# When the norms of the next units are made: at the end of a turn, or between its exponentials

## The chip, the cores and the metric

The kernel runs on one core of a Trainium2 chip. The core has five engines that work side by side, each through its own queue of instructions in a fixed order: TensorE (PE in the profile, matrix products), VectorE (DVE), ScalarE (ACT), GpSimd (POOL) and SyncE (SP, which here only starts DMAs). An instruction that waits holds up all that stands behind it in its own queue, and nothing in the others. The metric is the device time of one execution in microseconds (us); lower is better.

## The reference, cut to what matters

Two layers work on x, 8 sequences of 128 tokens with 512 features, in float32. The first is an adapter matrix chosen per sequence and a small mixture of low-rank experts. The second is attention over a paged cache of keys and values, followed by a router over 64 experts. Nearly all the time goes to the attention:

```python
q = jnp.einsum('bsd,ed->bse', x, Wq).reshape(bsz, seqlen, HQ, D)     # 32 heads of 128
k = jnp.einsum('bsd,ed->bse', x, Wk).reshape(bsz, seqlen, HK, D)     # 8 heads
...
q = _rmsnorm(q, q_norm_w)      # t * rsqrt(mean(t * t) + EPS) * w
k = _rmsnorm(k, k_norm_w)
...
q = _rope(q, pos)
k = _rope(k, pos)
...
scores = jnp.einsum('bqhd,bkhd->bhqk', q, k_all) * SCALE     # 512 cached keys and 128 new ones
scores = jnp.where(valid[:, None, None, :], scores, -1e+30)
probs = jax.nn.softmax(scores, axis=-1)
o = jnp.einsum('bhqk,bkhd->bqhd', probs, v_all)
```

The change is about the norms: for each query and key head the sum of squares over 128 features, and from it the factor `(mean + eps) ** -0.5`.

## The kernel before, in words

**Units and turns.** The attention is cut into 64 units: one sequence and one key head, with its four query heads. `iteration(u)` is one turn of the main loop, for u = 0 to 66, and works on several units at once, as a pipeline: it makes the scores and the softmax of unit u, the norms and the rotation of unit u + 3, the product with the values of unit u - 2 and the output product of unit u - 3. In between it makes the projections (queries, keys, values) of units further ahead. Four consecutive turns belong to one cycle of projections: in odd turns four products, in even turns three. In turns with u%4 = 2 the products of that turn complete unit u + 3 itself.

The order on each engine is written out by hand: the program is under a manual schedule, and each engine runs its instructions in the order in which the code issues them. The semaphore waits between engines follow from the tiles that the instructions share.

**One turn, by engine.** For each of the four heads h of unit u:

- TensorE makes `scores` (L798 against the cached keys, L801 against the new ones), then one output product of unit u - 3 (L902, into y), then a projection (L259).
- VectorE makes the masked maximum `mask_exp` (L811, from PSUM, scaled by the norm's factor `rs`), later the reciprocal of the softmax sum (L827) and the 32x32 block transpose of the normalized head (`blocks`, L833, into pb). It also adds the projection products (L262).
- ScalarE makes the exponential (L822, with the sum `den`).
- GpSimd multiplies with the reciprocal (`normalize`, L828). In the loop, `normalize(u, h - 1)` follows `mask_exp(u, h)`, so a head is normalized one step after its exponential, and `blocks(u, h - 2)` follows one step later.

**The end of a turn.** After the loop over heads come, in the order of the code: `add_output` (ya, L919 or L923), the mask of the next step, `heads_qk` (ScalarE, L867), the weight loads of some turns on GpSimd's queue (`load_q` L153, `load_o` L177), `normalize(u, 3)`, then `norms(u + 3)`, then the last two `blocks`, `exchange_out(u)` and `rotate(u + 3)`.

- `norms` has five squares on ScalarE (L308, one for each head, with its accumulator read), a copy of the values, vn (L310), and on GpSimd ss (L312, scale and add) and rs (L314, the power -0.5). There is one line for each: the profile names the tiles sq, vn, ss and rs.
- `exchange_out` sends the transposed blocks through DRAM (px), with two DMAs from SyncE's queue and two from ScalarE's (L847). In the next turn `exchange_in` fetches them back (qkb and pT, L857 and L860, SyncE). On SyncE's queue the rest of the key pages of the next step (kt, L194) stands behind that.
- `rotate` multiplies with the tables (L326, four query heads), and then the key head with its factor rs (L340), on VectorE; its result is transposed with the next unit's blocks (L784).
- In the next turn ScalarE begins with `evict_o` (oT, L891), the copy of the attention output of unit u - 2 out of PSUM, which TensorE needs for the first y product of that turn.

Some turns carry more: weight sums on VectorE in turns with u%16 from 10 to 13 (L163), weight loads on GpSimd's queue with u%16 = 8 to 11 (`load_q`, two DMAs each) and 12, 13 (`load_o`), four subtractions of x on GpSimd after turns 2, 5, 7 and 9 (`sums_x`). From turn 59 on the router of the finished sequences runs along (`f_turn`, a ScalarE copy at L686 behind the third exponential, and `f_gate`).

Of the kernel before, what the change touches and what calls it, by code (L numbers as in the profile page):

```python
# [9 lines left out]
F32 = mybir.dt.float32  # L10
# [6 lines left out]
P = 128  # L17
B = 8
# [5 lines left out]
D = 128  # L24
HKV, REP = 8, 4
NH = REP + 1
# [31 lines left out]
def adaln_ffn_kernel(  # L58
# [163 lines left out]
    pj = ctx.enter_context(tc.tile_pool(name="pj", bufs=1))  # L222
    units = [(st, st // B * GH + j) for st in range(NQ * B) for j in range(GH)]
    NU = len(units)
# [73 lines left out]
            )  # L298
        nc.scalar.copy(c_t[u][:, c * HW : (c + 1) * HW], ps)

    def norms(u):

        cs, b = c_t[u], units[u][0] % B
        ss = pj.tile([P, NH], F32, tag="ss", name=f"ss_{u}", bufs=5)
        sq = pj.tile([P, D], F32, tag="sq", name=f"sq_{u}")
        for h in range(NH):
            at = h // 2 * HW + h % 2 * D if h < REP else 2 * D
            nc.scalar.activation(sq, cs[:, at : at + D], AF.Square, accum_out=ss[:, h : h + 1])  # L308
        vn = pj.tile([P, D], F32, tag="vn", name=f"vn_{u}", bufs=6)
        nc.scalar.activation(vn, cs[:, 2 * HW - D :], AF.Copy, scale=down[:, b : b + 1])  # L310
        vn_t[u] = vn
        nc.gpsimd.tensor_scalar(ss, ss, 1.0 / D, eps[:, b : b + 1], ALU.mult, ALU.add)  # L312
        rs = pj.tile([P, NH], F32, tag="rs", name=f"rs_{u}", bufs=5)
        nc.gpsimd.tensor_tensor(rs, ss, mhalf, ALU.pow)  # L314
        rs_t[u] = rs
# [436 lines left out]
    with ExitStack() as l1:  # L752
# [223 lines left out]
        def iteration(u):  # L976

            on = lambda v: 0 <= v < NU
            fb = LAST.get(u)
            r, group = u % 16, (u // 16 + 1) * GH  # L980
            f = room(fb) if fb is not None else None

            if u % 4 == 3:
                k, j, four = (u + 5) // 4, 0, True
            elif u % 4 == 0:
                k, j, four = (u + 4) // 4, 0, False
            elif u % 4 == 1:
                k, j, four = (u + 3) // 4, 1, True
            else:
                k, j, four = (u + 2) // 4, 1, False  # L990
            slots = ()
            if 2 < u and k < NU // 4:
                slots = (1, 2, 6) if four else (4, 5, 3)
            st = u // GH
            pages = on(u) and 1 < st + 1 < NQ * B
            first, end = ((0, 10), (10, NPP))[u % GH]
            if pages:
                gather(st + 1, first, first + 3)
            if on(u - 1):
                exchange_in(u - 1)  # L1000
            if pages:
                gather(st + 1, first + 3, end)
            if pages:
                gather_v(st + 1, u % GH * LC // GH, (u % GH + 1) * LC // GH)
            if on(u + 3) and u % GH == 1:
                make_tables(units[u + 3][0])
            if u % GH == 0 and B <= st - 1 < NQ * B:
                load_y(st - 1)
            if on(u - 3):
                evict_o(u - 3)  # L1010
            if u >= NU and fb is not None:
                yT_t[fb] = f_turn(fb, *f)
            if u > NU:
                z = u - NU - 1
                z_turn(z, bank("q" if z else "kv", f"ztp_{z}"), lambda n, shape: y_home[
                    z
                ].rearrange("p (c s) -> p c s", c=NC))
            for h in range(REP):
                if on(u):
                    scores(u, h)  # L1020
                    mask_exp(u, h)
                    if h > 0:
                        normalize(u, h - 1)

                    if h == 1:
                        if u == 2:
                            rotate(4)
                        elif u == 3:
                            sums_q(1, 3, 2)
                        elif u == 4:  # L1030
                            sums_q(1, 4, 1)
                        elif r in (10, 11, 12, 13) and u < NU - 8:
                            sums_q(group + r // 12, *((3, 2), (4, 1))[r % 2])
                    if h == 2:
                        new_pb(u)
                        if u + 2 in range(3, NU):
                            blocks_qk(u + 2, u)
                    if h > 1:
                        blocks(u, h - 2)
                    if h == 1 and u == NU - 5:  # L1040
                        f_fold(f[1])
                    if h == 2 and fb is not None:
                        yT_t[fb] = f_turn(fb, *f)
                if on(u - 3):
                    output(u - 3, h)
                if h > 0 and slots:
                    project(k, j, slots[h - 1 : h])

                if (u, h) in WHOLE:
                    project_whole(1, *WHOLE[u, h])  # L1050
            if on(u - 3):
                add_output(u - 3)
            if on(u + 1) and (u + 1) % GH == 0:
                make_mask(units[u + 1][0])
            if u + 1 in range(3, NU):
                heads_qk(u + 1)

            if u < NU - 8:
                if r in (8, 9, 10, 11):
                    load_q(group + r // 10, r % 2, r % 2 + 2)  # L1060
                if r in (12, 13):
                    load_o(group, r % 2 * 2, r % 2 * 2 + 2)
            if 16 < u < NU and r in (1, 2):
                load_o(group - 1, r * 2 - 2, r * 2)
            if NU - 8 < u < NU - 2:
                f_weights(u - NU + 7)
            if u == 2:
                sums_q(0, 1)
            if on(u):
                normalize(u, REP - 1)  # L1070
            if u == 0:
                norms(4)
            elif 4 < u + 3 < NU:
                norms(u + 3)
            if on(u):
                blocks(u, REP - 2)
                blocks(u, REP - 1)
                exchange_out(u)
            if 4 < u + 3 < NU:
                rotate(u + 3)  # L1080
                if four and slots:
                    project(k, j, (7,))

            if u in (2, 5, 7, 9):
                sums_x({2: 2, 5: 3, 7: 0, 9: 1}[u])
            if u == NU - 14:
                t = wp.tile([P, 4 * DM], F32, tag="wo", name="y_home", bufs=GH + 1)
                y_home.update({b: t[:, b * DM : (b + 1) * DM] for b in range(4)})
            if u == NU - 6:
                rooms()  # L1090
            if fb is not None:
                f_gate(fb, *f_project(fb, yT_t.pop(fb), *f), *f)
            if on(u - 2):
                values(u - 2)
# [160 lines left out]
```

## Time and profile before

| | |
|---|---|
| time, median of 3 runs | 1243.18 us (1242.82 to 1249.42) |
| profiled execution, its own time | 1245.7 us |
| its span in the profile | 1243.9 us |
| TensorE busy | 1225.7 us (99%) |
| VectorE busy | 901.9 us (73%) |
| GpSimd busy | 590.9 us (48%) |
| ScalarE busy | 506.5 us (41%) |
| granted TensorE clock, mean | 0.998 |
| squares (L308), with reads | 98.8 + 59.7 us on ScalarE, 320 each |
| rs (L314) | 99.5 us on GpSimd, 64 instructions, 1554 ns mean |

A line of the timeline has the start and the duration in us, the engine, the line of the program, the operation, the tile written and the tiles read, the shape and the number of instructions; in brackets, the idle time before it and what ended it. A line of the waits has who waited (engine, tile, line), for whom, the total in us, how often, and the longest. "ACTq" and "SPq" are DMAs started from the queues of ScalarE and SyncE. An instruction's end, start plus duration, can lie a little past the start of the next one on its engine, because they are pipelined. Turns are counted by the masked maxima (L811), four to a turn; turn 20 starts at 439.47 us in this execution.

### The profile page before, as it was taken

The numbers are of one execution on the slowest core, as the hardware profiler recorded it, in microseconds if no ns is written. First come the engines' busy times: TensorE is split into PE (matmuls) and PEld (weight loads), VectorE is DVE, ScalarE is ACT, GpSimd is POOL, SyncE is SP. The second block draws the span as 40 slices with busy tenths as digits, with TensorE's granted clock in tenths as the row PEclk, the third lists the DMA queues.
The fourth block names the chain that finished last, engine by engine and source line by source line (L and its number), as shares of the span: only waits on it lengthen the run. The fifth ranks groups of instructions, "written<-read, shape, count | busy, mean of one in ns | idle before, by whom it ended". The sixth has DMA issues, their size and how long they took to land.

```text
span 1243.9 us, 15998 instructions
## 1 busy us (share of the span) xinstructions
PE 1225.7 (99%) x3847; PEld 651.1 (52%) x3847; DVE 901.9 (73%) x2045; ACT 506.5 (41%) x1457; POOL 590.9 (48%) x687
## 2 busy tenths in 40 slices
PE   8999899999999999999999999999999999999998
PEld 7765455554555555545555545554555555555444
DVE  3546788888877777788877777788777777777522
ACT  1334444444444444444444444444444444443211
POOL 2443565576544444565545545555555444543100
PEclk9999999999999999999999999999999999999999
DMA  8822777788877887788878878888888877787512
GB/s 302 304 78 94 229 234 245 245 274 281 269 243 245 272 258 239 259 295 278 269 248 267 264 221 258 294 272 267 257 268 262 255 243 233 246 261 269 179 51 85
DMA packets 205505, 298.99 MB, mean 240 GB/s; under 512 B 84643, under 2 KB 117156, under 8 KB 204516
## 3 DMA queue, kind: packets, MB, share of 16 engines
q1 hardware_dynamic: 173812, 205.58, 52.6%
q10 hardware_dynamic: 18720, 52.32, 12.0%
q0 software_dynamic: 12880, 40.08, 9.7%
q8 instruction: 31, 0.51, 0.2%
q14 instruction: 62, 0.51, 0.1%
HBM read 183.54 MB, written 114.36 MB: 239 GB/s over the span
## 4 chain that ended last, share of the span: by engine, by line
PE 89%; DMA 4%; DVE 2%; ACT 1%; issue 1%; POOL 1%; SPq 1%; ACTq 0%; DVEq 0%; POOLq 0%
PE o L880 19%; PE p L259 19%; PE y L902 17%; PE s L798 16%; PE s L801 4%; PE bp L517 2%; PE op L1147 2%; PE p L292 2%; PE cp L495 2%; PE fz L701 2%; DMA kt<-in_kc 1%; DMA bww<-in_base_w 1%; DMA px<-pb 1%; PE cp L512 1%; DMA pT<-px 1%
## 5 line engine op out<-in xcount | busy, mean ns | idle before, releaser
L828 POOL TENSOR_SCALAR p<-p,den 128x640 f32<-128x640 f32 x256 | 211.8, 827 | 424.4 <-DVE den L827 423.8
L822 ACT ACTIVATE p<-p,low 128x640 f32<-128x640 f32 x256 | 211.9, 828 | 436.3 <-DVE den L827 295.6
L811 DVE CUSTOM_DVE_ANT_0 p<-s,mask,rs 128x640 f32<-128x640 f32 x256 | 223.5, 879 | 108.8 <-PE s L801 106.1
L259 PE MATMUL p<-wqkv,xo 128*128 128x384 f32 x784 | 280.5, 487 | 0.0
L902 PE MATMUL y<-wo,oT 128*128 128x512 f32 x512 | 262.8, 598 | 7.6 <-ACT oT L891 7.4
L798 PE MATMUL s<-kt,qkT 128*128 128x512 f32 x504 | 258.9, 595 | 1.5 <-DVE low L811 0.8
L880 PE MATMUL o<-pT,vt 128*128 128x512 f32 x512 | 230.2, 593 | 0.0
L833 DVE STREAM_TRANSPOSE pb<-p 128x640 f32<-128x640 f32 x256 | 211.0, 824 | 16.9 <-POOL p L828 16.9
L259 PEld LDWEIGHTS p<-wqkv,xo 128*128 128x128 f32 x784 | 149.1, 190 | 139.8 <-issue 72.3
L801 PEld LDWEIGHTS s<-qkT 128*128 128x128 f32 x504 | 96.2, 191 | 121.0 <-issue 121.0
L880 PEld LDWEIGHTS o<-pT,vt 128*128 128x128 f32 x512 | 97.5, 190 | 110.1 <-issue 95.0
L204 POOL DMA_INDIRECT vt<-in_vc,vrow x128 | 136.3, 1065 | 37.4 <-issue 28.2
L798 PEld LDWEIGHTS s<-kt,qkT 128*128 128x128 f32 x504 | 95.4, 191 | 96.7 <-issue 54.0
L308 ACT ACTIVATE sq<-c 128x128 f32<-128x128 f32 x320 | 98.8, 309 | 8.1
L314 POOL TENSOR_TENSOR rs<-ss,mhalf 128x5 f32<-128x5 f32 x64 | 99.5, 1554 | 5.3
L801 PE MATMUL s<-qkT 128*128 128x128 f32 x504 | 97.2, 275 | 0.0
L891 ACT COPY oT<-o 128x512 f32<-128x512 f32 x64 | 37.4, 585 | 144.9 <-PE o L880 133.6
L902 PEld LDWEIGHTS y<-wo,oT 128*128 128x128 f32 x512 | 78.6, 192 | 14.2 <-ACT oT L891 9.7
L262 DVE TENSOR_TENSOR c<-c,p 128x384 f32<-128x384 f32 x84 | 45.3, 539 | 28.8 <-PE p L259 28.7
L880 PE MATMUL o<-pT,vn 128*128 128x512 f32 x128 | 65.4, 592 | 0.0
L308 ACT ACTIVATION_READ_ACCUMULATOR sq<-c 128x1 f32 x320 | 59.7, 187 | 0.0
L340 DVE SCALAR_TENSOR_TENSOR ca<-c,rs,tab 128x128 f32<-128x128 f32 x64 | 24.8, 387 | 45.1 <-POOL rs L314 45.1
(181 smaller groups left out, 1200.7 us busy)
## 6 DMA issues: line engine op xcount, KB each, us to landing
pT<-px SPq DMA_DIRECT2D x64, 1280.0 KB, 6.7
px<-pb ACTq DMA_DIRECT2D x120, 400.0 KB, 5.3
px<-pb SPq DMA_DIRECT2D x120, 400.0 KB, 5.5
qkb<-px SPq DMA_DIRECT2D x61, 320.0 KB, 3.5
kt<-in_kc SPq DMA_DIRECT2D x512, 32.0 KB, 4.4
wqkv<-in_wqkv POOLq DMA_DIRECT2D x32, 384.0 KB, 5.4
yd<-ya SPq DMA_DIRECT2D x24, 256.0 KB, 3.1
wo<-in_wo POOLq DMA_DIRECT2D x12, 512.0 KB, 4.7
```

Source lines behind the costliest of these rows:

```text
L204: nc.gpsimd.indirect_dma_start(out=kv_t[step][1][:, c, :], out_offset=None, in_=vc, in_offset=bass.IndirectOffsetOnAxis(ap=vrow[:, hf, at ...
L259: nc.tensor.matmul(out=ps, lhsT=xo[:, pr, x, c, :], rhs=w[:, c, :], start=(c == 0), stop=(c == 1))
L308: nc.scalar.activation(sq, cs[:, at : at + D], AF.Square, accum_out=ss[:, h : h + 1])
L314: nc.gpsimd.tensor_tensor(rs, ss, mhalf, ALU.pow)
L798: nc.tensor.matmul(out=s[:, :L], lhsT=qkT[:, h, :], rhs=kt[:, :, g % GH, :], start=True, stop=True)
L801: nc.tensor.matmul(out=s[:, L:NK], lhsT=qkT[:, h, :], rhs=qkT[:, REP, :], start=True, stop=True)
L811: nc.vector.tensor_tensor_reduce(out=p, in0=s_t.pop((u, h))[:, :NK], in1=mask_t[st], scale=rs_t[u][:, h : h + 1], scalar=BIG, op0=ALU.add, ...
L822: nc.scalar.activation(p, p, AF.Exp, bias=low, scale=-1.0, accum_out=den)
L828: nc.gpsimd.tensor_scalar(p_t[u, h], p_t[u, h], den, 1.0, ALU.mult, ALU.mult)
L833: nc.vector.transpose(pb_t[u][:, :, h * w : (h + 1) * w].rearrange("p i (j a) -> p j i a", a=32), p_t.pop((u, h)).rearrange("p (j i a) -> ...
L880: nc.tensor.matmul(out=o, lhsT=vt[:, c, j * D : (j + 1) * D] if c < LC else vn_t.pop(u), rhs=pT[:, c], start=(c == 0), stop=(c == LC),)
L902: nc.tensor.matmul(out=y_t[st], lhsT=oT_t[u][:, h, :], rhs=wo_t[g][:, h, :], start=(h == 0 and j == 0), stop=(h == REP - 1 and j == GH - 1),)
```

## The change

`norms` is split. `squares(u, first, end)` makes some of the five squares, and `norms(u, first)` makes the rest, vn, ss and rs. A flag `early` is set for turns u from 3 to 60 except those with u%4 = 2. In an early turn, three squares of unit u + 3 are issued behind the exponential of head 1, and the other two with vn, ss and rs behind that of head 2. Both stand ahead of the `normalize` call of that step, so on GpSimd ss and rs come between the normalizations of heads 0 and 1. In the turns with u%4 = 2, and outside the range, the norms stay at the end of the turn. No instruction is added or taken away, and the order on TensorE, VectorE and SyncE is the same as before; on ScalarE and GpSimd the moved instructions take their new places.

```diff
-    def norms(u):
-
-        cs, b = c_t[u], units[u][0] % B
-        ss = pj.tile([P, NH], F32, tag="ss", name=f"ss_{u}", bufs=5)
-        sq = pj.tile([P, D], F32, tag="sq", name=f"sq_{u}")
-        for h in range(NH):
+    ss_t = {}
+
+    def squares(u, first, end):
+
+        cs = c_t[u]
+        if first == 0:
+            ss_t[u] = pj.tile([P, NH], F32, tag="ss", name=f"ss_{u}", bufs=5)
+        ss = ss_t[u]
+        sq = pj.tile([P, D], F32, tag="sq", name=f"sq_{u}_{first}")
+        for h in range(first, end):
             at = h // 2 * HW + h % 2 * D if h < REP else 2 * D
             nc.scalar.activation(sq, cs[:, at : at + D], AF.Square, accum_out=ss[:, h : h + 1])
+
+    def norms(u, first=0):
+
+        squares(u, first, NH)
+        cs, b, ss = c_t[u], units[u][0] % B, ss_t.pop(u)
         vn = pj.tile([P, D], F32, tag="vn", name=f"vn_{u}", bufs=6)
...
+            early = 2 < u < NU - 3 and u % 4 != 2
...
                 if on(u):
                     scores(u, h)
                     mask_exp(u, h)
+
+                    if early and h == 1:
+                        squares(u + 3, 0, 3)
+                    elif early and h == 2:
+                        norms(u + 3, 3)
                     if h > 0:
                         normalize(u, h - 1)
...
             if u == 0:
                 norms(4)
-            elif 4 < u + 3 < NU:
+            elif 4 < u + 3 < NU and not early:
                 norms(u + 3)
```

## The prediction

> **What bounds the kernel now.** I read three views: the busy table, the list of waits, and one turn of the main loop instruction by instruction. The first two:
>
> ```profile
> PE 1225.7 (99%) x3847; PEld 651.1 (52%) x3847; DVE 901.9 (73%) x2045; ACT 506.5 (41%) x1457; POOL 590.9 (48%) x687
> ...
> PE y L902 <- ACT oT L891: 7.4, 8, 2.6
> ...
> DVE ca L340 <- POOL rs L314: 45.1, 59, 3.5
> ```
>
> TensorE is busy for 1225.7 of 1243.9 us, at a granted clock of 0.998. All its idle time is 18.2 us, and about half of that lies before the first turn and after the last. The waits to see: TensorE's largest is 7.4 us, in 8 pieces, for oT, the copy that ScalarE makes of the attention output. VectorE waits 45.1 us for rs, the result of the norms, but VectorE does not set the end. So the 45.1 us are worth at most what TensorE can recover: its stalls in turns 10, 26, 36, 44 and 59 are 0.73, 0.68, 0.96, 0.88 and 1.00, together 4.25 us, or 0.34%. The other question is whether the change makes TensorE wait where it doesn't now. Turn 20 (the iteration u = 20, without a stall), by engine: ScalarE and ACTq, TensorE, VectorE, GpSimd:
>
> ```profile
> 446.37 0.19 ACT L822 ACTIVATION_READ_ACCUMULATOR p<-p,low 128x1 f32 x1
> ...
> 453.05 0.84 ACTq L847 DMA_DIRECT2D px<-pb  x2
> 454.31 0.58 ACT L891 COPY oT<-o 128x512 f32<-128x512 f32 x1 [1.29 <-PE o L880]
> ...
> 455.19 1.02 PE L902 MATMUL y<-wo,oT 128*128 128x512 f32 x2
> ...
> 448.78 0.83 DVE L833 STREAM_TRANSPOSE pb<-p 128x640 f32<-128x640 f32 x1
> 450.02 0.56 DVE L262 TENSOR_TENSOR c<-c,p 128x384 f32<-128x384 f32 x1 [0.42 <-PE p L259]
> ...
> 451.10 0.15 DVE L827 RECIPROCAL den<-den 128x1 f32<-128x1 f32 x1
> ...
> 452.17 0.85 DVE L833 STREAM_TRANSPOSE pb<-p 128x640 f32<-128x640 f32 x1 [0.18 <-POOL p L828]
> ...
> 448.95 0.80 POOL L828 TENSOR_SCALAR p<-p,den 128x640 f32<-128x640 f32 x1 [2.45 <-DVE den L827]
> ```
>
> See the order on ScalarE at the turn's end: the exchange DMAs wait for the last block transpose (452.17), take 0.84, and behind them in the same queue stands oT, for which the y matmul at 455.19 waits. From the transpose: 0.88 to the DMAs, 0.88 more to where oT may start (453.93), but it starts at 454.31, when TensorE has finished o: 0.38 free. In turn 10, where y did stall, it began 0.64 after oT:
>
> ```profile
> 287.46 0.85 ACTq L847 DMA_DIRECT2D px<-pb  x2
> 288.35 0.58 ACT L891 COPY oT<-o 128x512 f32<-128x512 f32 x1 [1.17 <-PE s L801]
> ...
> 288.99 1.13 PE L902 MATMUL y<-wo,oT 128*128 128x512 f32 x2 [0.73 <-ACT oT L891]
> ```
>
> In turn 20 that would be 454.95, and y comes at 455.19: another 0.24 free. **An even turn therefore stands 0.62 us of delay of its last block transpose**; beyond that each tenth is TensorE time. An odd turn has one more product (1.29 us) ahead of o; in turn 9 its DMAs are out at 269.53 and oT starts at 271.30, so 1.77 us are free.
>
> **The change, part by part.** It adds no instruction and removes none. In turns 3 to 60 except those with u%4 = 2 (44 turns; 15 even, 29 odd) it moves 5 squares with 5 accumulator reads and the vn copy on ScalarE, and ss and rs on GpSimd. The queues of TensorE, VectorE and SyncE keep their order; the moved steps issue no DMA.
>
> *ScalarE.* A square with its read follows the next by 0.43 us, so three cost 1.30 after the second exponential, two and vn (0.39) cost 1.25 after the third. In turn 20 the second exponential ends at 443.32 and the third starts at 445.63 (2.3 us gap); the third ends at 446.56, the fourth starts at 449.16 (2.6 us gap). Both fit: nothing. In odd turns the copy of u (L265, 0.48) waits behind the three squares, about 1.1 us later; its reader at L262 comes 3.0 us after it today (turn 21): nothing. What the squares free at the end of the turn (2.1 us before the exchange DMAs) is gained only where ScalarE, not the transpose, held the DMAs: turn 59.
>
> *GpSimd, where the price is.* ss waits for the fifth square, and behind it now stand the normalizations of heads 1, 2 and 3, the weight DMAs, and behind those VectorE's transposes. In turn 20: third exponential read out at 446.56, two squares to 447.31, ss at 447.41 (0.10 later, as at the end of turns today), 0.27 long, rs 0.09 later, at 447.77. How long is rs in that place? The trace has it beside other work:
>
> ```profile
> 127.26 0.27 POOL L312 TENSOR_SCALAR ss<-ss,eps 128x5 f32<-128x5 f32 x1 [1.45 <-ACT sq L308]
> 127.61 1.18 POOL L314 TENSOR_TENSOR rs<-ss,mhalf 128x5 f32<-128x5 f32 x1
> ...
> 519.19 1.74 POOL L314 TENSOR_TENSOR rs<-ss,mhalf 128x5 f32<-128x5 f32 x1
> ```
>
> The first runs beside two masked maxima (L811), the second beside the two rotations L326, which have two inputs in SBUF. Ends: 1.18 and 1.75. In the new place it meets an L262 add and the fourth masked maximum, then an idle VectorE; no L326. I take 1.20. The Trainium skill, "SBUF — State Buffer", section "SBUF: two separate sides", says that GpSimd and such a two-input VectorE instruction take a shared port pair as a lock: the first to start keeps it for its whole length, the other is blocked. At 519.19 rs had started 0.03 before the first L326, yet the two L326 kept their pace (0.57 apart) and rs was drawn out by 0.54. So the measurement decides: beside L326 it is rs that pays. Were the fourth masked maximum, due at 447.90, held by rs as that rule has it, it would end at 449.77, and the transpose behind it would start at 449.85; by the rows it starts at 449.80. The sum is the same within 0.05.
>
> With 1.20, rs ends at 448.97 and head 1's normalization runs to 449.77 instead of 446.50. The transpose of head 1 (448.78) starts at 449.80, 1.02 late. It ends its 0.75 pitch at 450.55; the L262 add due at 450.02, where it had waited 0.42 for TensorE, is 0.53 late, and so are ya, the reciprocal (451.63), head 3's normalization (0.24 behind it, 0.80 long) and the last transpose: 452.70. Head 2's normalization is done at 450.57 and waits on nothing. **Delay of the last transpose 0.53, against 0.62: no stall, by 0.09.** Seven of the exchange DMA pairs took 0.88 to 0.96 instead of 0.84; I allow 0.3 us in all for edges like these.
>
> Then rotate: 452.70 + 0.77 + 0.57 + 0.68 = 454.72 for L340, no longer waiting for rs. Turn 24, which is regular, has it 15.22 after its first masked maximum, which in turn 20 is 454.69. The removed wait (about 0.5) is eaten by the added one.
>
> *Turns that differ.* u = 8, 24, 40: two weight DMAs (1.56 us) stand between the normalizations of heads 2 and 3. Turn 24: head 2 ends at 516.83, the DMAs at 518.36, head 3 at 519.21; last transpose 519.25 against 518.45, 0.80 late: 0.18 over, three times, +0.5. Turns 11 and 13, with weight sums on VectorE: 1.3 late, oT 0.15 to 0.18 later, inside 0.24: nothing. Turns 59 and 60 have another ScalarE copy (L686) behind the third exponential; it comes 1.25 late, its matmul had 0.6 to spare: +0.6 each. But turn 59's stall of 1.00 comes from squares, rs (1.67 us of VectorE waiting) and the gate behind it, and goes: together +0.2. Turn 9 ends with four GpSimd subtractions beside L340, which then takes 0.82 instead of 0.35; they start earlier now, and turn 10's stall may lose 0.3.
>
> *SyncE.* Its exchange DMAs come 0.5 to 1.3 later, and behind them in the next turn the last three K pages. Their landing against the first scores: 0.1 us to spare in turns 25 and 49, 1 to 4.6 in the other turns behind a moved even one where the trace shows it. At most 0.5 in each of the two: +0.6 as a middle. The transposed probabilities are needed 15 us after they land: nothing.
>
> **Sum:** 0.3 + 0.5 + 0.2 - 0.3 + 0.6 = +1.3 us. The profiled execution took 1245.7 us for a span of 1243.9; both grow alike, so I add it to the median, 1243.2: **1244.5 us**.
>
> **Rivals.** *Faster:* the early norms relieve turns 10, 26, 36, 44 and 59 of all 4.25 us, which gives 1239. For it: 45 us of VectorE waiting. Against: in 26, 36 and 44 the exchange DMAs are slow or wait for pages, which no norm changes. *Slower, by one mechanism:* rs stays near 1.75 in its new place (the profile's mean is 1.554, with L326 nearly always beside it). Then the last transpose is 1.03 late, and each even turn loses 0.41 (8 x 0.41), turns 8, 24, 40 0.74 each, turns 12, 28, 44 some 1.8 together, odd turns 11, 13, 29, 43 another 1.8, and turn 10 0.5 more: +9.6, 1252.8. It decides from rs above about 1.3 us. *Slower by pages:* with landings of 7.4 us, as in turn 49, in place of about 5, all 14 turns that follow a moved even turn lose about 0.5: 1250.
>
> **Chances.** Within 0.5% (6.2 us; runs of one kernel here spread by as much, 1242.82 to 1249.42): 0.79, my forecast, with the faster rival's 1239 inside it. Slower: 0.17, of which rs 0.11 and pages or what I don't see 0.06. Faster by over 0.5% needs more stalls removed than I can find: 0.04. Range 1240 to 1251: most of the faster rival, the page case, the lower part of the rs case.
>
> **What would show it.** Right: rs near 1.20 us; head 1's transpose waiting about 1 us for GpSimd in place of L340's wait for rs; the last transpose some 0.5 us later against y; TensorE's wait for oT still near 7 us. Wrong: rs at 1.6 or more, or y waiting for oT in most even turns, or scores waiting for pages.

## The result, and the profile after

The changed kernel takes 1251.09 us (median of 8 runs, 1249.23 to 1253.04) beside 1246.35 us for the kernel before, run alongside (8 runs, 1241.68 to 1249.42). The ratio is 1.0049, with a 95% interval of 1.003 to 1.0068. A second measurement gave 1.0057 (1.0037 to 1.0077). So the change costs about 0.5%, some 5 to 7 us, where 1.3 us were forecast. 1251.09 lies just above the range on record (1240 to 1251). The kernel before was itself 3.2 us slower in these runs than in the three shown ahead of the prediction. The difference is therefore the better measure of the forecast, and it is wrong by 3.4 us or more.

The profiled execution took 1249.23 us for a span of 1247.5, at a granted clock of 0.997. Before, these were 1245.7, 1243.9 and 0.998. The line numbers after are higher by 9 from `norms` on: the square is L312, rs is L323, the masked maximum is L820, `normalize` is L837, the block transpose is L842, the exchange is L856, oT is L900 and y is L911.

First the page of the changed kernel: the busy table, and from the costliest groups the two kinds of matmul that can wait at a turn's edge.

```profile
PE 1228.7 (98%) x3847; PEld 651.5 (52%) x3847; DVE 915.9 (73%) x2045; ACT 497.0 (40%) x1457; POOL 580.8 (47%) x687
...
L911 PE MATMUL y<-wo,oT 128*128 128x512 f32 x512 | 263.8, 600 | 6.4 <-ACT oT L900 6.4
L807 PE MATMUL s<-kt,qkT 128*128 128x512 f32 x504 | 258.9, 595 | 3.8 <-DMA kt<-in_kc 2.4
```

Then its list of waits, the two rows that the change exchanges, with the first of them as it was before, and the durations of rs in the view of that tile:

```profile
DVE pb L842 <- POOL p L837: 53.3, 103, 1.8
...
DVE ca L349 <- POOL rs L323: 13.1, 16, 3.7
```

```profile
DVE pb L833 <- POOL p L828: 16.9, 65, 2.2
```

```profile
L323 POOL TENSOR_TENSOR rs<-ss,mhalf x64: 1183/1197/1744, 66.8 to 1119.0; 128x5 f32<-128x5 f32 x64
```

The reader is to see three things. VectorE's wait for rs fell from 45.1 to 13.1 us, and its wait for a normalized head grew to 53.3 us (16.9 before). The median rs is 1.197 us (minimum, median and maximum stand in ns). And TensorE's wait for oT is 6.4 us, not more than the 7.4 of before. In this one execution it has a new wait instead, 2.4 us for key pages.

Turn 20 again, instruction by instruction; it starts at 441.36 us here. The last row is the first o matmul of the same turn before:

```profile
449.63 1.19 POOL L323 TENSOR_TENSOR rs<-ss,mhalf 128x5 f32<-128x5 f32 x1
...
450.83 1.57 POOL L837 TENSOR_SCALAR p<-p,den 128x640 f32<-128x640 f32 x2
...
451.66 0.84 DVE L842 STREAM_TRANSPOSE pb<-p 128x640 f32<-128x640 f32 x1 [0.91 <-POOL p L837]
451.71 3.60 PE L889 MATMUL o<-pT,vt 128*128 128x512 f32 x8
...
454.54 0.84 DVE L842 STREAM_TRANSPOSE pb<-p 128x640 f32<-128x640 f32 x1 [0.19 <-POOL p L837]
...
455.41 0.85 ACTq L856 DMA_DIRECT2D px<-pb  x2
...
456.31 0.59 ACT L900 COPY oT<-o 128x512 f32<-128x512 f32 x1 [4.00 <-PE o L889]
...
457.08 1.02 PE L911 MATMUL y<-wo,oT 128*128 128x512 f32 x2
```

```profile
449.82 3.60 PE L880 MATMUL o<-pT,vt 128*128 128x512 f32 x8
```

rs takes 1.19 and the two normalizations of heads 1 and 2 run behind it; head 1's transpose waits 0.91 for them. The last transpose starts 2.83 after the first o matmul; before it was 2.35 (452.17 less 449.82). It is 0.48 late. oT starts 4.60 after o where it was 4.49, and y doesn't wait. This is the chain of the prediction, with 0.48 for its 0.53.

Where, then, does TensorE lose the time? A turn is taken from the start of its last o matmul to that of the next: 15.92 us into an even turn and 17.21 into an odd one, when nothing waits. What is above that, in us, in the two profiled executions, is put down to the turn that it leads into, so that the stalls which the prediction names at the end of turns 10, 26, 36 and 44 stand here at 11, 27, 37 and 45:

| place | before | after |
|---|---|---|
| turn 3, while the pipeline fills | 5.32 | 6.47 |
| turns 9, 25, 41 (behind u = 8, 24, 40) | 0 | 0.79 |
| turns 12, 30, 38 (in after, waits for key pages) | 0.43 | 3.09 |
| turns 13, 29 (behind u = 12, 28; y waits for oT) | 0.24 | 1.06 |
| turns 11, 27, 37, 45, 58 (y waits for oT) | 4.67 | 3.96 |
| turns 59 and 60 | 3.45 | 2.79 |

What else turns 4 to 58 lose is 0.45 and 0.26 in all. The regular even turns have 0.00 in both. Turn 28, which leads into turn 29, is not regular: on VectorE it carries weight sums. After, then before:

```profile
584.74 3.60 PE L889 MATMUL o<-pT,vt 128*128 128x512 f32 x8
...
588.11 0.84 DVE L842 STREAM_TRANSPOSE pb<-p 128x640 f32<-128x640 f32 x1 [0.19 <-POOL p L837]
...
590.62 1.12 PE L911 MATMUL y<-wo,oT 128*128 128x512 f32 x2 [0.34 <-ACT oT L900]
```

```profile
583.29 3.60 PE L880 MATMUL o<-pT,vt 128*128 128x512 f32 x8
...
585.65 0.84 DVE L833 STREAM_TRANSPOSE pb<-p 128x640 f32<-128x640 f32 x1 [0.19 <-POOL p L828]
```

The last transpose starts 3.37 behind o where it was 2.36, so it is 1.01 late and not 0.48; in turn 12 it is 0.93 late. Both are more than the 0.62 that turn 20 has to spare. The other larger pieces of after (in turn 12 the wait is one for pages too, 0.62):

```profile
607.53 1.10 PE L807 MATMUL s<-kt,qkT 128*128 128x512 f32 x2 [0.52 <-DMA kt<-in_kc]
...
741.54 1.10 PE L807 MATMUL s<-kt,qkT 128*128 128x512 f32 x2 [1.24 <-DMA kt<-in_kc]
...
856.50 0.84 DVE L842 STREAM_TRANSPOSE pb<-p 128x640 f32<-128x640 f32 x1 [0.19 <-POOL p L837]
...
858.16 1.65 ACTq L856 DMA_DIRECT2D px<-pb  x2
859.85 0.59 ACT L900 COPY oT<-o 128x512 f32<-128x512 f32 x1 [4.58 <-DVE sa L349]
...
860.49 1.12 PE L911 MATMUL y<-wo,oT 128*128 128x512 f32 x2 [2.06 <-ACT oT L900]
```

At 858.16, the end of turn 44, the two exchange DMAs start 1.66 after their transpose, not 0.87, and take 1.65, not 0.85; oT stands behind them and y waits 2.06. (The releaser that the row of oT names, sa, isn't one it needs: the DMAs ahead of it in ScalarE's queue hold it.) Slow exchanges of this kind are not new. The kernel before has six pairs over 1.2 us in its profile; this is the one at the end of turn 36:

```profile
719.45 2.59 ACTq L847 DMA_DIRECT2D px<-pb  x2
722.07 0.58 ACT L891 COPY oT<-o 128x512 f32<-128x512 f32 x1 [2.93 <-PE s L801]
...
722.71 1.13 PE L902 MATMUL y<-wo,oT 128*128 128x512 f32 x2 [0.96 <-ACT oT L891]
```

They come mostly in even turns, but not in the same ones in every execution: in the 18 profiles of this case, a pair of over 1.5 us on one of the two queues ends turn 44 in fifteen, turn 50 in twelve, turns 26 and 36 in eleven, turn 42 in ten, and 26 more turns in eight or fewer. Single runs of the kernel before spread from 1241.8 to 1254.8 us (63 runs on one chip), about twice the effect looked for. A sum over two executions, such as the table, can therefore name places but can't carry a difference of 0.5%; that is left to medians, below.

### The profile page after: what moved, and what is told of

The parts are those of the page before. It is cut to its first block, busy times and chain, and to the rows that moved or that the text cites. A ratio compares the mean times of both kernels' runs of the same rounds, so it can differ in the third digit from the quotient of the medians.

```text
span 1247.5 us, 15985 instructions
## 1 busy us (share of the span) xinstructions
PE 1228.7 (98%) x3847; PEld 651.5 (52%) x3847; DVE 915.9 (73%) x2045; ACT 497.0 (40%) x1457; POOL 580.8 (47%) x687
## 4 chain that ended last, share of the span: by engine, by line
PE 82%; DMA 5%; DVE 4%; ACT 3%; POOL 2%; issue 2%; SPq 1%; ACTq 0%; DVEq 0%; POOLq 0%
PE o L889 18%; PE p L259 17%; PE y L911 15%; PE s L807 15%; PE s L810 4%; PE bp L526 2%; PE op L1162 2%; PE cp L504 2%; PE fz L710 2%; PE p L292 2%; DMA kt<-in_kc 2%; ACT p L831 1%; ACT sq L312 1%; DMA px<-pb 1%; DMA pT<-px 1%
## 5 line engine op out<-in xcount | busy, mean ns | idle before, releaser
L837 POOL TENSOR_SCALAR p<-p,den 128x640 f32<-128x640 f32 x256 | 213.9, 838 | 266.3 <-DVE den L836 263.8
L820 DVE CUSTOM_DVE_ANT_0 p<-s,mask,rs 128x640 f32<-128x640 f32 x256 | 223.2, 878 | 92.7 <-PE s L810 91.2
L911 PE MATMUL y<-wo,oT 128*128 128x512 f32 x512 | 263.8, 600 | 6.4 <-ACT oT L900 6.4
L842 DVE STREAM_TRANSPOSE pb<-p 128x640 f32<-128x640 f32 x256 | 211.7, 827 | 53.4 <-POOL p L837 53.3
L204 POOL DMA_INDIRECT vt<-in_vc,vrow x128 | 141.3, 1104 | 84.2 <-PE o L889 57.5
L900 ACT COPY oT<-o 128x512 f32<-128x512 f32 x64 | 37.5, 586 | 238.8 <-PE o L889 223.9
L321 POOL TENSOR_SCALAR ss<-ss,eps 128x5 f32<-128x5 f32 x64 | 17.4, 272 | 185.0 <-ACT sq L312 185.0
L312 ACT ACTIVATE sq<-c 128x128 f32<-128x128 f32 x320 | 97.6, 305 | 6.7
L323 POOL TENSOR_TENSOR rs<-ss,mhalf 128x5 f32<-128x5 f32 x64 | 83.9, 1310 | 5.3
L911 PEld LDWEIGHTS y<-wo,oT 128*128 128x128 f32 x512 | 78.8, 193 | 13.2 <-ACT oT L900 8.6
L793 DVE STREAM_TRANSPOSE pb<-ca 128x640 f32<-128x640 f32 x60 | 49.9, 832 | 17.7 <-DMA px<-pb 16.1
```

The lines of the kernel that those rows point to most:

```text
L204: nc.gpsimd.indirect_dma_start(out=kv_t[step][1][:, c, :], out_offset=None, in_=vc, in_offset=bass.IndirectOffsetOnAxis(ap=vrow[:, hf, at ...
L820: nc.vector.tensor_tensor_reduce(out=p, in0=s_t.pop((u, h))[:, :NK], in1=mask_t[st], scale=rs_t[u][:, h : h + 1], scalar=BIG, op0=ALU.add, ...
L837: nc.gpsimd.tensor_scalar(p_t[u, h], p_t[u, h], den, 1.0, ALU.mult, ALU.mult)
L842: nc.vector.transpose(pb_t[u][:, :, h * w : (h + 1) * w].rearrange("p i (j a) -> p j i a", a=32), p_t.pop((u, h)).rearrange("p (j i a) -> ...
L911: nc.tensor.matmul(out=y_t[st], lhsT=oT_t[u][:, h, :], rhs=wo_t[g][:, h, :], start=(h == 0 and j == 0), stop=(h == REP - 1 and j == GH - 1),)
```

## The experiments

Three theories. **Delay:** the last transpose is 0.5 us late, and this costs TensorE time at y, although the regular turn has 0.62 to spare. **Pages:** the later exchange makes key pages late. **Early work:** the squares, vn or the rest of the new order cost something by themselves. All ratios are to the kernel before, run alongside, with the 95% interval, from five rounds each.

**The change again**, without an edit.

> The changed kernel a second time, to see what of its cost comes back. Theory 1 (order on GpSimd): rs ahead of three normalizations makes the last block transpose late, so that y waits for oT in the loaded even turns and the last key pages land late; then 1.003 to 1.007 of the kernel before, with the 0.25 us steps of turns 8, 24 and 40 again, y waits in turns 12, 28 and 44 again, and one to four waits for key pages of 0.5 to 1.5 us, though not in the same turns. Theory 2 (nothing but luck in DMA landings and the clock): 0.998 to 1.002.

1.0057 (1.0037 to 1.0077). The cost is real.

**The delay alone.** The kernel before, with VectorE held up ahead of the fourth reciprocal in the 44 turns by a mask that is computed once more, with the same values:

```diff
+            if 2 < u < NU - 3 and u % 4 != 2:
+                v = st + 1 if u % GH else st
+                nc.vector.tensor_scalar(
+                    mask_t[v], kidx, lenf[:, v % B : v % B + 1], MASKED, ALU.is_ge, ALU.mult
+                )
```

> The kernel before, its norms left at the end of the turn, but with the mask of the step computed a second time (0.47 us on VectorE) ahead of the fourth reciprocal in the same 44 turns: nothing but a last transpose that is about 0.5 us late. Theory 1 (the late transpose is the cost): 1.003 to 1.006, like the change, with y waits in the even turns and some for pages. Rival (the cost is in something else that the change moves: gathers and tables that start earlier on GpSimd, or the squares): 0.999 to 1.001.

1.0030 (1.0016 to 1.0044), 3.7 us. In turn 20 its last transpose starts 2.82 after the first o matmul, as in the changed kernel, and the regular even turns lose 0.00 as there. So a delay of 0.47 that no regular turn shows costs 0.3% by itself. Where, its profile doesn't show. The y waits that were expected in the even turns aren't there, and its largest new wait is one of the scores for the exchange, at the start of turn 30:

```profile
PE y L902 <- ACT oT L891: 3.6, 4, 2.4
...
PE s L798 <- DMA px<-pb: 3.4, 1, 3.4
```

Nor is it the delay of the change in every turn. In turns 12 and 28 this transpose is 0.47 late as well, where the change makes it 0.93 and 1.01.

**Twice the delay.** The same with that mask computed twice more (`for _ in range(2)` around it), in the same turns.

> The kernel before with the mask computed twice more than needed in the 44 turns: the last transpose 0.94 us late instead of 0.47 (which cost 1.003). If TensorE pays what goes beyond the 0.62 us that an even turn stands, 0.3 us in each of 15 even turns come on top: 1.006 to 1.009, with a step of 0.2 to 0.4 us in most moved even turns. If the 1.003 came from something else in that kernel: 1.003 to 1.004.

1.0104 (1.0076 to 1.0133), above the 1.009 expected at most. Its list of waits, and turn 20:

```profile
PE y L902 <- ACT oT L891: 13.8, 20, 2.9
```

```profile
456.39 3.60 PE L880 MATMUL o<-pT,vt 128*128 128x512 f32 x8
457.66 1.13 DVE L1072 TENSOR_SCALAR mask<-kidx,lenf 128x640 f32<-128x640 f32 x2
...
459.79 0.85 DVE L833 STREAM_TRANSPOSE pb<-p 128x640 f32<-128x640 f32 x1 [0.18 <-POOL p L828]
...
461.55 0.59 ACT L891 COPY oT<-o 128x512 f32<-128x512 f32 x1 [1.96 <-PE o L880]
...
462.19 1.13 PE L902 MATMUL y<-wo,oT 128*128 128x512 f32 x2 [0.27 <-ACT oT L891]
```

The last transpose is now 3.40 behind o, 1.05 later than before. Less the 0.62 that the prediction found free, 0.43 are left; the turn is 0.53 longer, and so are the turns into 5, 17, 21, 49, 53 and 57. The slack of a regular turn was read rightly. Beyond it nearly every moved even turn pays, as the prediction's slower rival has it, only that rs isn't what brings the kernel there.

**The delay taken away.** In the change, `norms` goes one call later, behind head 1's normalization:

```diff
-                    elif early and h == 2:
-                        norms(u + 3, 3)
                     if h > 0:
                         normalize(u, h - 1)
+                    if early and h == 2:
+                        norms(u + 3, 3)
```

> The change with one call moved: ss and rs behind the normalization of head 1 instead of ahead of it; squares, vn and all else as in the change. In turn 20 of before that gap lasts from 446.50 to 448.95, and rs would end at 448.97. Theory 1 (rs ahead of that normalization makes the last transpose late): the transposes are on time, 0.999 to 1.002 of the kernel before, without the 0.25 us steps of turns 8, 24 and 40. If early squares or early rs cost by themselves: 1.003 to 1.005.

1.0024 (1.0007 to 1.004). Turn 20 of this kernel, then its list of waits:

```profile
450.11 1.19 POOL L323 TENSOR_TENSOR rs<-ss,mhalf 128x5 f32<-128x5 f32 x1
...
451.14 0.82 DVE L842 STREAM_TRANSPOSE pb<-p 128x640 f32<-128x640 f32 x1
...
452.19 3.60 PE L889 MATMUL o<-pT,vt 128*128 128x512 f32 x8
...
454.54 0.84 DVE L842 STREAM_TRANSPOSE pb<-p 128x640 f32<-128x640 f32 x1 [0.19 <-POOL p L837]
```

```profile
PE y L911 <- ACT oT L900: 5.2, 5, 2.7
```

Head 1's transpose no longer waits, and the last one is 2.35 behind o, exactly as before the change. The turns behind u = 8, 24 and 40 lose nothing again. About 0.3% of the 0.5 are gone. The result lies between what the two theories expected, and the intervals overlap (up to 1.0040 here; from 1.0030 and 1.0037 for the change), so the size is less sure than the direction.

**Early squares, late factors.** In two kernels ss and rs are split off from `norms`, as `factors`; the squares and vn stay early. In the first, `factors` is at the end of the turn, in its old place; in the second it is behind head 2's normalization, but at the end in turns with u%16 from 8 to 13.

```diff
+    def factors(u, ss=None):
...
             elif 4 < u + 3 < NU and not early:
                 norms(u + 3)
+            elif early:
+                factors(u + 3)
```

> The change with only its ScalarE half: squares and vn between the exponentials, but ss and rs at the end of the turn, behind the fourth normalization, where they were. Theory 1: the transposes of head 1 no longer wait for GpSimd, and the cost goes: 0.997 to 1.001 of the kernel before. Rival (the squares between the exponentials cost by themselves, in turns 59 and 60 or elsewhere): 1.003 to 1.006, like the whole change.

> The change with ss and rs behind the normalization of head 2, in GpSimd's gap ahead of that of head 3 (1.59 us wide in turn 20 of before, against 1.56 for ss and rs); in turns with weight DMAs or weight sums (turn modulo 16 from 8 to 13) at the end of the turn. Theory 1: early factors without a late transpose, 0.996 to 1.000. Rival (early factors are bad wherever they stand, because GpSimd then builds its tables beside the rotation on VectorE): 1.002 to 1.005.

1.0019 (1.0002 to 1.0037) and 1.0016 (0.9999 to 1.0034). Both are without the late transpose, both are below the change, and neither is faster than before; both lie between what was expected with and without a cost of the squares. VectorE's wait for rs is 13 us in these two as well, and the 32 us that went bring nothing. What is left, about 0.2%, as with rs behind head 1, is small against the noise: the intervals start at 1.0002 and 0.9999.

**Halves of the change.** `early` only where u%4 = 0, or only where u is odd:

```diff
-            early = 2 < u < NU - 3 and u % 4 != 2
+            early = 2 < u < NU - 3 and u % 4 == 0
```

```diff
-            early = 2 < u < NU - 3 and u % 4 != 2
+            early = 2 < u < NU - 3 and u % 2 == 1
```

> Early norms only in turns with u%4 = 0 (15 of the 44). Theory 1: the y waits are all in these turns (0.25 us in turns 8, 24, 40, some 0.3 to 1 in 12, 28, 44), and the pages that come late are those behind the exchange of these turns: 1.002 to 1.005, nearly all of the cost. Rival (each early turn costs alike): a third of it, 1.001 to 1.002.

> Early norms only in odd turns (29 of the 44). Theory 1 (late last transpose): an odd turn has some 2 us to spare before its y product and loses about 0.5 to 1.3 of them, so little: 1.000 to 1.002 of the kernel before, without the 0.25 us steps of turns 8, 24 and 40. Rival (each early turn costs alike): two thirds of the cost, 1.003 to 1.004.

Even turns alone: 1.0039 (1.0022 to 1.0055). Odd turns alone: 1.0029 (1.0015 to 1.0042), a miss, since up to 1.002 was expected and the prediction has nothing for them. In its profile turn 13, one of those with weight sums, ends like this:

```profile
338.57 2.58 ACTq L856 DMA_DIRECT2D px<-pb  x2
341.19 0.59 ACT L900 COPY oT<-o 128x512 f32<-128x512 f32 x1 [6.14 <-DVE ca L353]
...
341.82 1.13 PE L911 MATMUL y<-wo,oT 128*128 128x512 f32 x2 [1.76 <-ACT oT L900]
```

The prediction has that turn 1.3 late with 1.77 free. An exchange of 2.58 in place of 0.84 uses up all of it and 1.3 more. In the regular odd turn nothing is lost.

**Pages first.** In the change, all six key pages of an odd turn are issued ahead of `exchange_in`:

```diff
+            if pages and u % GH:
+                gather(st + 1, first + 3, end)
             if on(u - 1):
                 exchange_in(u - 1)
-            if pages:
+            if pages and u % GH == 0:
                 gather(st + 1, first + 3, end)
```

> The change, with all six key pages of an odd turn issued ahead of the two loads of the exchange on SyncE's queue, instead of three of them behind. Theory 1a (late pages are half of the cost): 1.001 to 1.003 of the kernel before, and no wait for pages at the scores. Theory 1b (the y product behind the exchange DMAs is nearly all of the cost): 1.004 to 1.006, as for the change.

1.0065 (1.0042 to 1.0088). Its waits:

```profile
PE y L911 <- ACT oT L900: 10.4, 11, 2.5
```

No score waits for pages any more, and the kernel is no faster. The 2.4 us of page waits in the changed kernel's profile are thus not a part that can be taken out to get the time back. The edit also puts six page issues ahead of the exchange on SyncE, so it isn't a clean removal of one wait.

**oT first.** If the DMAs ahead of oT are the trouble, oT can go ahead of them: in moved even turns ScalarE's two exchange DMAs are issued behind `evict_o`. This was run on top of the pages-first kernel, and then alone.

```diff
-                    (nc.sync if n else eng).dma_start(
-                        out=m[:, :, i, n:end].rearrange("k b f -> b k f"),
-                        in_=src[i * 32 : (i + 1) * 32],
-                    )
+                    go = lambda q=(nc.sync if n else eng), o=m[:, :, i, n:end], s=src[
+                        i * 32 : (i + 1) * 32
+                    ]: q.dma_start(out=o.rearrange("k b f -> b k f"), in_=s)
+                    if i < QD // 2 or u % 4 or not 2 < u < NU - 3:
+                        go()
+                    else:
+                        held.append(go)
...
+            if on(u - 3):
+                evict_o(u - 3)
+            for go in held_t.pop(u - 1, ()):
+                go()
```

> The order with all pages first in odd turns (measured at 1.0065), and besides, in turns with u%4 = 0, ScalarE's two exchange DMAs issued behind the copy oT instead of ahead of it. If the cost is paid where oT stands behind the exchange DMAs: the y waits at the end of these turns go, with the 0.25 us steps, and 2 to 5 us of time, 1.002 to 1.005. If it is paid elsewhere: 1.006 to 1.008.

> The change, with ScalarE's two exchange DMAs issued behind the copy oT in turns with u%4 = 0; pages in their old order. If the cost is paid at the y product of these turns: 1.001 to 1.004, without the 0.25 us steps; if the exchange, now later, makes pages or qkT late instead: 1.005 or more, with waits of the scores for DMAs.

With pages first: 1.0043 (1.003 to 1.0055), below the 1.0065 of pages first alone, though the intervals overlap. Alone: 1.0116 (1.0085 to 1.0147), far slower than the change. The waits of the latter:

```profile
PE y L916 <- ACT oT L905: 5.0, 6, 2.8
PE s L807 <- DMA kt<-in_kc: 4.5, 5, 1.8
PE s L807 <- ACT oT L905: 2.4, 3, 1.1
```

Half the exchange now comes after oT, so the pages behind it on SyncE come later too: 4.5 us in 5 waits. The page rival is right in this: there is a point from which a later exchange makes pages late, and it is not far beyond the change.

**Value gathers and tables later.** The diff is that of the third kernel here, the change itself with `gather_v` and `make_tables` moved from the start of a turn to behind head 0's normalization. The same move was made on the kernel with the factors in the gap, on the kernel before, and on the one with rs behind head 1; and once with the gathers alone, on the factors in the gap.

```diff
-            if pages:
-                gather_v(st + 1, u % GH * LC // GH, (u % GH + 1) * LC // GH)
-            if on(u + 3) and u % GH == 1:
-                make_tables(units[u + 3][0])
...
                         normalize(u, h - 1)
+                    if h == 1 and pages:
+                        gather_v(st + 1, u % GH * LC // GH, (u % GH + 1) * LC // GH)
+                    if h == 1 and on(u + 3) and u % GH == 1:
+                        make_tables(units[u + 3][0])
```

> The order with ss and rs in the gap ahead of the fourth normalization, and besides the gathers of values and the tables on GpSimd moved from the start of a turn behind the normalization of head 0, so that they run neither beside the exchange DMAs nor beside the rotation. If the gathers that start earlier are what makes the exchange DMAs take 2 us and more in that order: 0.995 to 0.999 of the kernel before. If they have nothing to do with it: 1.000 to 1.003, as without the move.

> The kernel before, with the gathers of values and the tables on GpSimd moved behind the normalization of head 0; the norms stay at the end of the turn. A control: there the gathers start behind ss and rs, after the exchange DMAs are out. Theory (two causes: a late transpose, and gathers that start beside the exchange DMAs): 0.998 to 1.001, since neither cause is there to be removed. If the move gains by itself, whatever the norms do: 0.994 to 0.998.

> The change as it is, with the gathers and tables moved behind the normalization of head 0. Theory (two causes that add up): the late transpose stays, the gathers no longer run beside the exchange DMAs, 1.002 to 1.004 of the kernel before, with the 0.25 us steps of turns 8, 24 and 40. If the late transpose is the whole cost: 1.004 to 1.006. If the gathers are: 0.999 to 1.001.

> The order with ss and rs in the gap (1.0016, and 0.9999 with gathers and tables moved), with only the gathers moved behind the normalization of head 0 and the tables left at the start of the turn. If the gathers beside the exchange DMAs were its loss: 0.999 to 1.001. If the tables beside the rotation were: 1.001 to 1.003.

> As the order with ss and rs behind head 1's normalization, with gathers and tables moved behind that of head 0. The move alone was 0.9984 on the kernel before and took 0.001 to 0.002 off two other orders: 0.997 to 1.001 here. If early factors are worth something once they delay nothing: below 0.998.

| kernel | without the move | with it |
|---|---|---|
| before | 1 | 0.9984 (0.9963 to 1.0004) |
| factors in the gap | 1.0016 | 0.9999 (0.9984 to 1.0014) |
| factors in the gap, gathers alone | 1.0016 | 0.9997 (0.9979 to 1.0016) |
| change | 1.0049 and 1.0057 | 1.0046 (1.003 to 1.0062) |
| rs behind head 1 | 1.0024 | 1.0020 (1.0002 to 1.0038) |

The move gains up to 0.19%, with the gathers alone as with both, and the kernel before gains nearly as much; no single gain is clear of the noise. The last order was expected at 1.001 at most and missed it. So the move tells little about the change, and what the gathers hold up at the start of a turn isn't settled here. The kernel before with late gathers is the best of all, 1242.91 us, but its interval still holds 1. No kernel was found that clearly beats the one before.

**The same turns in every profile.** A sum over one execution can't carry 0.5%, but a loss that stands in the same turn of every kernel with one order, and in none with the other, isn't luck. What turns lose above 15.92 or 17.21, from one profile of each kernel:

| kernel | turns 9, 25, 41 | turns 13, 29 | turn 30 | turns 59, 60 |
|---|---|---|---|---|
| before | 0 | 0.24 | 0 | 3.44 |
| before, late gathers | 0 | 0 | 0 | 1.73 |
| delay alone | 0.07 | 0.03 | 5.37 | 2.05 |
| change | 0.79 | 1.06 | 0.76 | 2.80 |
| even turns alone | 0.74 | 0.99 | 0.92 | 2.71 |
| change, late gathers | 1.77 | 1.61 | 0 | 2.80 |
| rs behind head 1 | 0 | 0.40 | 0.99 | 2.80 |
| factors at the end | 0 | 0 | 1.18 | 2.80 |
| factors in the gap | 0 | 0 | 0.67 | 2.80 |

The turns of the first two columns lose most where rs makes the last transpose late. (The 1.77 has a slow exchange in it, at the end of turn 8; the 0.24 of before has one too.) Turn 30 waits for key pages where the squares of the even turns are early and gathers and pages keep their places; with late gathers, and with pages first, it doesn't. What makes these pages late isn't shown. (The 5.37 is the wait for the exchange above.) In turns 59 and 60 the early squares make the router's copy late, and its matmul waits; in the changed kernel:

```profile
1101.94 1.10 PE L701 MATMUL fr<-fw,rooms 128*128 128x64 f32 x8 [0.25 <-ACT rooms L695]
...
1119.31 1.10 PE L701 MATMUL fr<-fw,rooms 128*128 128x64 f32 x8 [0.28 <-ACT rooms L695]
```

With norms at the end in both turns this matmul waits in no profile, and turns 59 and 60 lose at least 0.83 and 0.90; with early norms in both they lose 1.35 and 1.45. So the early squares do cost something by themselves, about 1.1 us here. The 3.44 of before has a stall of 1.00 at y that the two other orders with late norms don't have.

## Why the prediction was wrong

The mechanism was right: rs at 1.20, a chain that makes the last transpose late, and a regular even turn that hides it. What failed is the part on the turns that differ. Its slack was that of turn 20, and its gains were stalls of one execution.

- **rs at 1.20: right.** Its median is 1.197. The slower rival rests on 1.75 and falls. That its 1252.8 lies close to the 1251.09 is luck, though its price for a transpose that is about 1 us late, +9.6 us, is of the size that the doubled delay showed (0.0104 of 1246.44, 13 us).
- **Last transpose 0.53 late, 0.62 free, no stall in a regular even turn: right.** It is 0.48, and these turns lose 0.00; the doubled delay confirmed the 0.62.
- **u = 8, 24, 40, +0.5: right in place, a little small.** They lose 0.25, 0.29 and 0.25. Of the 0.25, the prediction has 0.18 as the excess; the rest is like the 0.1 by which the doubled delay's turn (0.53) exceeded its excess (0.43).
- **Turns 12, 28 and 44, at nothing: this is the step that failed.** I found turns 11 and 13 to be 1.3 late because of their weight sums, but the even turns that carry the same sums are in the slower rival only, not in my own sum. In the changed kernel their transpose is 0.8 to 1.0 us late, beyond 0.62. The turns behind u = 12 and 28 lose 0.45 and 0.61 there, 0.43 and 0.56 with even turns alone, 0.78 and 0.83 with late gathers. Behind u = 44 it is 0.74 in that last kernel, where its exchange took 0.79; in the changed kernel a slow exchange covers it up.
- **Turns 59 and 60, +0.2: the other step that failed.** The +0.6 for each was nearly right, since they lose 0.52 and 0.55 more with early norms. But the 1.00 that I took off was a stall of one execution, and can't be set against a cost that always comes: +1.1.
- **Pages, +0.6: of the right size, in another turn.** The changed kernel's profile has 2.4 us of waits for pages, of which only the one in turn 30 comes back in the other orders, as a loss of 0.67 to 1.18. Its pages are fetched in turn 29, where I had counted 1 to 4.6 us to spare; turns 25 and 49, which I called tight, show none. The medians don't show a gain from taking these waits out.
- **Turn 10, -0.3: not seen.** Turn 11 loses 1.00 before and 0.94 after.
- **"I allow 0.3 us in all for edges like these": not settled.** The same profile has six exchange pairs over 1.2 us on ScalarE's queue, up to 2.62, and I named the stalls they make only as something that the change might relieve. That a late transpose is dear where the exchange is slow is argued, not shown: the number of slow exchanges can't be set from the program, and in the profile of the delay alone turns 29, 37 and 45 lose 1.24 in all, less than the 2.72 of before.
- **"Odd turns: nothing": also wrong.** Alone they cost 1.0029. Of that the 0.5 of turn 59 comes back in every profile. Turn 13 shows how a slow exchange can use up the slack, but such exchanges are rare in odd turns, so the rest is open. Even and odd halves add up to more than the whole, within their intervals.

As an estimate from these profiles, the places that come back make 0.8 (behind u = 8, 24, 40), about 1.8 (behind 12, 28, 44), 1.1 (turns 59 and 60) and 0.8 (turn 30), together 4.5 us, beside 4.7 and 7.2 in the two measurements. With rs off the path the last two remain, 1.7 to 2.3 us or 0.14 to 0.18%; measured were 0.16 to 0.24 in the three kernels of that kind.

**What stays open:** the 3.7 us of the delay alone, most of the odd turns' 0.29%, and what the second measurement has above 4.5 us. The further 1.15 us in turn 3 goes with the granted clock, as the last section shows, and it isn't known whether the change has a part in that.

## What to carry to other kernels

Slack read from a regular turn of one execution is the slack of that kind of turn. Before a term is put at nothing, go through every kind of turn that carries other work, and redo the sum there. A stall seen in one execution is not yet a gain: look for it in a second one before it is set against a cost. A producer taken out of one engine's wait and set ahead of another's work doesn't vanish; placed one call later, behind the piece that the critical transpose waits for, it cost about half as much. An engine that waits 45 us on something nobody else waits for has nothing to give.

## What the runs showed of the hardware

**Some work of VectorE and GpSimd is drawn out side by side, some isn't.** The power rs takes 1.20 beside a masked maximum, which keeps its pace too: in turn 20 after, one starts at 449.80, 0.17 behind rs, and takes 0.87, and all 256 take 0.84 to 0.89. So rs doesn't hold it, as the prediction considered for a moment. Beside the rotations L326 it takes 1.74, as in the row at 519.19, and they keep theirs (medians 0.65 and 0.68). In early even turns GpSimd has no rs to make at the end, and starts the next turn's two tables (L233) sooner, so that they now meet the rotation, in the changed kernel's turn 20:

```profile
456.74 0.92 DVE L349 SCALAR_TENSOR_TENSOR sa<-c,rs,tab 128x128 f32<-128x128 f32 x1
457.44 0.80 POOL L233 TENSOR_TENSOR tab<-nw,cos 128x256 f32<-128x256 f32 x1
457.69 0.92 DVE L352 TENSOR_TENSOR ca<-ca,sa 128x320 f32<-128x320 f32 x1
458.21 0.99 POOL L233 TENSOR_TENSOR tab<-nw,sin 128x256 f32<-128x256 f32 x1
458.53 1.02 DVE L353 TENSOR_TENSOR ca<-ca,sa 128x320 f32<-128x320 f32 x1
```

Before, VectorE's three took 0.35, 0.49 and 0.48, and the tables 0.75 and 0.74. The next turn's first masked maximum starts 18.11 after this turn's, where it was 17.29 (439.47 to 456.76); TensorE didn't wait for it.

**Starting a DMA isn't a fixed price.** The pair of exchange DMAs takes 0.84 us on ScalarE's queue in the regular turn. In others it took up to 2.62 on ScalarE's and 2.63 on SyncE's queue in the kernel before, up to 1.65 and 3.42 in the changed one, and up to 3.4 and 4.3 in the other kernels.

**A short stall costs more than the wait that is shown.** A wait of 0.27 at y made the turn 0.53 longer, one of 2.06 made it 2.33 longer, and the 0.25 and 0.28 of the router's matmul made it 0.52 and 0.55. At the first long wait of the loop, 2.61 us before and 2.31 after, the granted clock falls. Windows of before, then of after, with the clock behind the busy times:

```profile
150.00:160.00 10.00, 7.39 (x17) 3.62 (x18) 6.25 (x11) 4.43 (x16) 7.26 (x9) 0.83 1.00 256
```

```profile
150.00:160.00 10.00, 7.68 (x15) 3.68 (x14) 6.37 (x10) 4.62 (x17) 7.42 (x9) 0.66 0.99 249
```

From 160 us on it is 1.00 again in both. What turn 3 loses goes with it: in the 18 profiles it is 5.0 to 5.9 us where the clock of this window is 0.83, and 6.5 to 7.9 where it is 0.66 to 0.73. The wait alone doesn't decide it. In one kernel (rs behind head 1, late gathers) the clock stayed at 1.00 behind a wait of 2.60, and turn 3 lost 3.5.
